# A four-layer graph attention kernel: the adjacency mask turned by DMA, and its value test moved to layer 2

## The chip, the core and the metric

The kernel runs on one core of a Trainium2 chip. The core has a matrix engine (TensorE, PE in the profile), a vector engine (VectorE, DVE), an activation engine (ScalarE, ACT), a general engine (GpSimd, POOL) and a queue engine that only issues transfers (SyncE, SP). Each engine works off its own list of instructions in order, and waits on semaphores where an instruction needs another engine's result. Transfers between the chip's main memory (HBM) and the on-chip memory (SBUF) are done by 16 DMA engines. Matrix products land in a small accumulator memory (PSUM). The metric is the device time of one launch in microseconds (us), the median of several runs.

## What is computed

Sixteen graphs of 1024 nodes with 256 features each pass through four attention layers. All four layers use the same adjacency matrix of its graph. It is symmetric, has ones on its diagonal and is sparse otherwise, with int32 entries of 0 and 1. In a shortened form:

```python
x: (16, 1024, 256) float32;  adj: (16, 1024, 1024) int32
for layer in 0, 1, 2:                       # each with its own W, a
    h = maximum(layernorm(x), 0)
    Wh = h @ W
    e = act(Wh @ a1 [:, :, None] + Wh @ a2 [:, None, :])
    weights = where(adj != 0, exp(+-e), 0); normalised by row
    x = x + post(weights @ Wh)              # post: identity, elu, elu
h = maximum(layernorm(x), 0)                # layer 3: four heads of 64
e_h = leaky_relu(src_h[:, :, None] + dst_h[:, None, :])   # where adj == 1
att = softmax over edges
y = relu(att @ h_h + bias) + h_h; normalised per head, * gamma + beta
x = x + y
```

Layer 3 of the reference has separate vectors for edge types 1 to 5. The fast path of the kernel covers adjacency values of 0 and 1 only. It therefore tests every entry, and a general path, which is compiled into the same program, runs if the test fails.

## The kernel before

**Tiling.** A graph is one batch. Its 1024 nodes are NI = 8 blocks of P = 128 rows; node 128 i + p lies in block i at partition p. The features x_b of a batch stay in SBUF for all four layers.

**The mask.** `load(b)` (L96) prepares a batch. SP loads x_b (L99). For each block i, POOL issues a transfer that loads 128 rows of the adjacency and casts int32 to bf16 on the way (L106). ACT takes (a - 1/2) squared of each entry and sums it by row (L117); a row of only zeros and ones sums to N/4, and a larger sum is found at the end of the kernel (L530 to L532). TensorE then transposes the eight 128x128 squares of the block into a PSUM tile called misc (L122), and ACT copies this to the byte mask (L123). The mask has the sources j at the partitions, in blocks j, and the targets along the row. The matrix is symmetric in this data, but the kernel doesn't use that. The mask is loaded AHEAD = 2 blocks ahead, from a pool of three buffers.

**A layer.** `project` (L233) normalises two node blocks at a time: statistics and subtraction on DVE (L239, L240, L244), the inverse root on POOL (rstd, L227), transposes on TensorE (L252), a copy to SBUF on ACT (hT, L254), then the projection (L259). What comes out is evicted to V by ACT (L320, L322) and DVE (L324), in layer 3 to h3, ex and V3 by ACT and POOL (L340 to L348). `weigh` (L268) makes the attention weights of a layer or head: TensorE spreads one value per node over a row of all partitions (L276), and then one DVE instruction per source block j (L280) compares the row with a value per partition and multiplies by the mask of block j. Exponentials are taken per node and not per edge, so this instruction is all the work there is per edge. `attend` (L352) multiplies weights with V (L367) for each target block i, and its `finish` adds the result to x_b: in layers 1 and 2 by an exponential on ACT (L303), three DVE instructions (L295, L296, L305, L306 in all) and an addition on POOL (L307). Layer 3 multiplies per head in halves of 512 targets (L471), copies the sums (L481), transposes them (L486), and normalises y per head on DVE, ACT and POOL (L431 to L446). The output leaves by SP (L502).

**The order of the work.** Everything is written as Python generators, and each `yield` hands a planned cost back. Two streams exist, one of the even and one of the odd batches. The loop at L520 always continues the stream with the smaller sum; the second begins LAG = 120 units later. So a batch's layers interleave with those of another batch, which is about half a batch away. Inside layer 3 of batch b, `next(coming)` (L482) takes one step of `load(b + 2)` after each half of a head. On top of this written order, the build places instructions on each engine by its own estimate of when they become ready, so that an engine's list can differ from the order of the code. Once built, the lists are fixed.

The few lines that set the loads' place are these:

```python
        for i in range(AHEAD):
            fetch(i)
        yield
        for i in range(NI):
            if i + AHEAD < NI:
                fetch(i + AHEAD)
            adj_i = fetched.pop(i)
            ...
            yield
```

Of the kernel before, what the change touches and what calls it, by code (L numbers as in the profile page):

```python
# [32 lines left out]
F32 = mybir.dt.float32  # L33
BF = mybir.dt.bfloat16
U8 = mybir.dt.uint8
I16 = mybir.dt.int16
I32 = mybir.dt.int32
AF = mybir.ActivationFunctionType
ALU = mybir.AluOpType
AX = mybir.AxisListType  # L40

P = 128
# [17 lines left out]
def short_path(ctx: ExitStack, tc: tile.TileContext, ins: dict, out: bass.AP, bad: bass.AP):  # L60

    nc = tc.nc
    x, adj = ins["x"], ins["adj"]
    B, N, D = x.shape
    H, T, E = ins["L3_a_src"].shape
    NI = N // P
    NK = D // P
    HALF = 512
    NH = N // HALF
    NG = HALF // P  # L70
    EXT = [3, 3, 3, 3 * H]
    AHEAD = 2
    LAG = 120.0

    const = ctx.enter_context(tc.tile_pool(name="const", bufs=1))
    nodes = ctx.enter_context(tc.tile_pool(name="nodes", bufs=3))
    adjs = ctx.enter_context(tc.tile_pool(name="adjs", bufs=3))
    wide = ctx.enter_context(tc.tile_pool(name="wide", bufs=2))
    psum = ctx.enter_context(tc.tile_pool(name="psum", bufs=2, space=bass.MemoryType.PSUM))

    ident = const.tile([P, P], F32, name="ident")
    make_identity(nc, ident)
    ident_b = const.tile([P, P], BF, name="ident_b")
    nc.vector.tensor_copy(ident_b, ident)
    minus_half = const.tile([P, 1], F32, name="minus_half")
    nc.vector.memset(minus_half, -0.5)
    ones = const.tile([P, P], F32, name="ones")
# [2 lines left out]
    squares = const.tile([P, B, NI], F32, name="squares")  # L90
    inverses = const.tile([P, B, NI], F32, name="inverses")


    xs, masks = {}, {}

    def load(b: int):  # L96

        xs[b] = nodes.tile([P, NI, D], F32, name="x_b")
        nc.sync.dma_start(xs[b], x[b].rearrange("(i p) f -> p i f", p=P))  # L99
        mask = masks[b] = nodes.tile([P, NI, N], U8, name="mask")  # L100
        fetched = {}

        def fetch(i: int):

            fetched[i] = adjs.tile([P, N], BF, name="adj_i")
            nc.gpsimd.dma_start(fetched[i], adj[b, ts(i, P), :])  # L106

        for i in range(AHEAD):
            fetch(i)
        yield  # L110
        for i in range(NI):
            if i + AHEAD < NI:
                fetch(i + AHEAD)
            adj_i = fetched.pop(i)

            every = wide.tile([P, N], BF, name="wide")
            nc.scalar.activation(  # L117
                every, adj_i, AF.Square, bias=minus_half, accum_out=squares[:, b, i : i + 1]
            )
            turned = psum.tile([P, NI, P], BF, name="misc")  # L120
            for j in range(NI):
                nc.tensor.transpose(turned[:, j, :], adj_i[:, ts(j, P)], ident_b)  # L122
            nc.scalar.copy(mask[:, :, ts(i, P)], turned)  # L123
            yield

    edges = ctx.enter_context(tc.tile_pool(name="edges", bufs=NI))
# [8 lines left out]
    bias = const.tile([P, D], F32, name="bias")  # L135
# [94 lines left out]
    def accumulator(b: int) -> bass.AP:  # L230
        return psum.tile([P, HALF], F32, name=f"acc{b % 2}")
# [36 lines left out]
    def weigh(b: int, column, c, op, into: list):  # L268


        while row_taken:
            yield 0.25
        row_taken.append(b)
        r = psum.tile([P, N], F32, name="row", bufs=1)
        for i in range(NI):
            nc.tensor.transpose(r[:, ts(i, P)], column(i).to_broadcast([P, P]), ident)  # L276
        yield 0.5
        for j in range(NI):
            w = edges.tile([P, N], F32, name=f"weights{b % 2}")
            nc.vector.scalar_tensor_tensor(w, r, c(j), masks[b][:, j, :], op0=op, op1=ALU.mult)  # L280
            into.append(w)
            if j == NI - 1:
                row_taken.pop()
            yield 0.5

    def start(behind, b: int):

        for t in behind:
            if row_taken == [b]:
                return  # L290
            yield t
# [17 lines left out]
    def batch(b: int):  # L309
        xb = xs.pop(b)  # L310
        if b == 0:
            next(preparing)
        coming = load(b + 2) if b + 2 < B else iter(())

        def begin(l: int):

            V = nodes.tile([P, NI, H, E + 1], F32, name="V", bufs=4).rearrange("p i h e -> p i (h e)")

            def evict(i: int, projected: bass.AP, rstd: bass.AP):
                nc.scalar.activation(V[:, i, D : D + 3], projected[:, D:], AF.Exp, scale=rstd)  # L320
                if l == 2:
                    nc.scalar.mul(V[:, i, :D], projected[:, :D], rstd)  # L322
                else:
                    nc.vector.tensor_scalar(  # L324
                        V[:, i, :D], projected[:, :D], rstd, V[:, i, D : D + 1],
                        op0=ALU.mult, op1=ALU.mult,
                    )

            return V, evict

# [3 lines left out]
        def begin3():  # L334
            h3 = last["h3"] = single.tile([P, NI, D], F32, name="h3")
            V3 = nodes.tile([P, NI, H, E + 1], F32, name="V", bufs=4)
            ex = last["ex"] = small.tile([P, NI, 3 * H], F32, name="ex", bufs=2)
# [14 lines left out]
        def attend(l: int, V: bass.AP, finish, then: int):  # L352

            weights = []
            behind = weigh(
                b, lambda i: V[:, i, D + 2 : D + 3], lambda j: V[:, j, D + 1 : D + 2],
                ALU.min if l == 1 else ALU.max, weights,
            )
            yield from start(behind, b)
            following = begin(then) if then < 3 else begin3()  # L360
            steps = iter(())
            accs = {}

            def product(i: int, j: int):
                if j == 0:
                    accs[i] = accumulator(b)[:, : D + 1]
                nc.tensor.matmul(  # L367
                    accs[i], weights[j][:, ts(i, P)], V[:, j, : D + 1],
                    start=(j == 0), stop=(j == NI - 1),
                )  # L370


            for j in range(NI):
                next(behind)
                product(0, j)
                product(1, j)
                yield 0.9
            for _ in behind:
                pass
            for i in range(NI):  # L380
                if i > 1:
                    for j in range(NI):
                        product(i, j)
                acc = accs.pop(i)
                finish(i, acc)
                if i != 0:
                    yield 3.6
                if i % 2 == 1:

                    yield from steps  # L390
                    steps = project(b, then, xb, i // 2, following[1])
                yield from islice(steps, 1)
            yield 1.0
            yield from steps
            return following[0]
# [8 lines left out]
        def finish(i: int, acc: bass.AP):  # L404
            add_elu(xb[:, i, :], acc)
# [6 lines left out]
        for steps in pairs:  # L412
            yield from steps
        if b == 0:
            for _ in chain(loading, preparing):
                pass
        V = yield from attend(0, V, finish0, 1)
        V = yield from attend(1, V, finish, 2)
        V3 = yield from attend(2, V, finish, 3)


        h3, ex = last["h3"], last["ex"]
        y = single.tile([P, NI, H, E], F32, name="y")
        normed = []
        shape = [P, NI, E]

        def center(h: int):

            yh = y[:, :, h, :]
            head = ts(h, E)  # L430
            nc.gpsimd.tensor_add(yh, yh, bias[:, head].unsqueeze(1).to_broadcast(shape))  # L431
            nc.vector.scalar_tensor_tensor(yh, yh, 0.0, h3[:, :, head], op0=ALU.max, op1=ALU.add)
            mean = small.tile([P, NI], F32, name="mean")
            nc.vector.tensor_reduce(mean, yh, AX.X, ALU.add)
            nc.vector.tensor_scalar_mul(mean, mean, 1.0 / E)
            nc.vector.tensor_sub(yh, yh, mean.unsqueeze(2).to_broadcast(shape))
            square = wide.tile(shape, F32, name="wide")
            nc.scalar.activation(square, yh, AF.Square)
            var = small.tile([P, NI], F32, name="var")
            nc.vector.tensor_reduce(var, square, AX.X, ALU.add)  # L440
            return yh, head, inverse_root(var, NI, L3_EPS, 1.0 / E)
# [18 lines left out]
        for n in range(H * NH):  # L460
            h, g = divmod(n, NH)
# [37 lines left out]
            pass  # L499
        rescale(*normed.pop())  # L500
        for g in range(NH):
            nc.sync.dma_start(  # L502
                out[b, ts(g, HALF), :].rearrange("(i p) f -> p i f", p=P),
                y[:, ts(g, NG)].rearrange("p i h e -> p i (h e)"),
            )
        yield 1.0

# [1 line left out]
    def stream(first: int):  # L509
# [3 lines left out]
        for b in range(first, B, 2):  # L513
            yield from batch(b)

    loading, preparing = load(0), prepare()
    next(loading)
    next(preparing)
    streams = [[0.0, stream(0)], [LAG, stream(1)]]
    while streams:  # L520
        ahead = min(streams, key=lambda s: s[0])
        t = next(ahead[1], None)
# [381 lines left out]
```

## Time and profile before

| what | value |
|---|---|
| median of three runs | 3197.18 us (3196.29 to 3198.49) |
| the profiled execution's own time | 3197.01 us |
| its span, first to last instruction | 3195.3 us |
| mean granted TensorE clock | 0.991 |
| DMA moved | 72.09 MB, mean 23 GB/s |
| HBM read, written | 86.38 MB, 16.78 MB |
| L122 TensorE, mask transposes | 1024 x, 84.2 us busy, 222 ns each |
| L117 ACT, Square of a block | 128 x, 1142 ns and 190 ns for the sum's read-out |
| L123 ACT, mask copies | 128 x, 1011 ns |
| L106 POOL, issue of a load | 128 x, 605 ns; 3.8 us from issue to landing |
| L280 DVE, weights | 896 x, 1275 ns |

How to read it: the page gives the busy time of each engine over the span, and then groups of equal instructions by line with their mean time. A group is followed by the time in which its engine stood idle just before it, and by what ended that idle time. An engine's busy share is an average over stages with different limits. Matmuls are pipelined, so that the durations of single ones overlap.

### The profile page before, as it was taken

The page shows a single profiled execution, that of the slowest core. Times are in us where ns is not written, and L with a number is a line of the kernel's source. Part 1 is how long each engine was busy: PE and PEld are TensorE (multiplying, and loading weights), DVE is VectorE, ACT ScalarE, POOL GpSimd, SP SyncE. Part 2 cuts the span into 40 slices and gives each one's busy share as a digit, 9 for nine tenths or more (in the row PEclk, how much of TensorE's full clock was granted, in tenths as well). Part 3 has the DMA queues.
Part 4 walks back from the last instruction along what each step waited for, and adds up shares of the span by engine and source line. Part 5 has one row for each costly group of instructions (what it writes and reads, how often), then busy time and mean ns, then how long its engine had stood idle before and what let it go on. Part 6 is the DMA issues. An engine that isn't in the chain of part 4 may idle for free.

```text
span 3195.3 us, 37581 instructions
## 1 busy us (share of the span) xinstructions
PE 3058.6 (96%) x13702; PEld 2112.1 (66%) x13702; DVE 2370.9 (74%) x5244; ACT 855.3 (27%) x1857; POOL 1002.4 (31%) x1286
## 2 busy tenths in 40 slices
PE   7899999999999999999999999999999999999987
PEld 5666776667666686666867667676676767766552
DVE  5576778777787767787687876878768787677756
ACT  3322223222232312323123231232313222232120
POOL 1223324232242322423224232342323323233332
PEclk8999999999999999999999999999999999999998
DMA  4101101111010100101001010111101111000000
GB/s 107 24 7 17 34 4 21 34 20 30 7 37 18 28 19 11 44 11 43 1 14 40 14 40 1 17 37 17 37 1 20 34 17 37 4 14 14 1 14 14
DMA packets 55951, 72.09 MB, mean 23 GB/s; under 512 B 5072, under 2 KB 38992, under 8 KB 55760
## 3 DMA queue, kind: packets, MB, share of 16 engines
q0 software_dynamic: 18432, 33.56, 6.9%
q1 hardware_dynamic: 37328, 36.05, 3.5%
q8 instruction: 111, 1.82, 0.2%
q14 instruction: 80, 0.66, 0.1%
HBM read 86.38 MB, written 16.78 MB: 32 GB/s over the span
## 4 chain that ended last, share of the span: by engine, by line
PE 71%; DVE 17%; POOL 6%; ACT 2%; issue 2%; DMA 1%; ACTq 0%; POOLq 0%; SPq 0%; DVEq 0%
PE acc L367 32%; PE acc L471 21%; PE acc L259 12%; DVE weights L280 8%; PE misc L252 2%; PE row L276 2%; POOL rstd L227 2%; POOL y L431 1%; POOL x_b L307 1%; PE misc L122 1%; DVE centered L244 1%; DVE stats L239 1%; DVE above L305 1%; ACT below L303 1%; PE misc L486 1%
## 5 line engine op out<-in xcount | busy, mean ns | idle before, releaser
L367 PE MATMUL acc<-V,weights 128*128 128x257 f32 x6144 | 1449.8, 384 | 41.9 <-DVE weights L280 20.3
L367 PEld LDWEIGHTS acc<-V,weights 128*128 128x128 f32 x6144 | 1143.8, 191 | 352.3 <-DVE weights L280 99.4
L471 PE MATMUL acc<-weights,V 128*65 128x512 f32 x2048 | 960.6, 593 | 1.9 <-DVE weights L280 1.7
L280 DVE SCALAR_TENSOR_TENSOR weights<-row,ex,mask 128x1024 f32<-128x1024 f32 x512 | 626.9, 1275 | 18.7 <-PE row L276 11.3
L259 PE MATMUL acc<-W,hT 128*128 128x259 f32 (+1 forms) x2048 | 521.7, 392 | 38.0 <-ACT hT L254 22.8
L471 PEld LDWEIGHTS acc<-weights,V 128*65 128x65 f32 x2048 | 272.4, 138 | 354.3 <-issue 311.5
L227 POOL TENSOR_TENSOR rstd<-rstd,minus_half 128x2 f32<-128x2 f32 (+1 forms) x320 | 301.0, 943 | 645.6 <-DVE rstd L226 632.0
L280 DVE SCALAR_TENSOR_TENSOR weights<-row,V,mask 128x1024 f32<-128x1024 f32 x384 | 474.5, 1275 | 33.4 <-PE row L276 32.9
L259 PEld LDWEIGHTS acc<-W,hT 128*128 128x128 f32 x2048 | 378.4, 191 | 170.7 <-ACT hT L254 60.0
L307 POOL TENSOR_TENSOR x_b<-x_b,above 128x256 f32<-128x256 f32 x256 | 191.1, 751 | 813.6 <-DVE above L306 731.1
L303 ACT ACTIVATE below<-acc,inv 128x256 f32<-128x256 f32 x256 | 120.3, 474 | 756.3 <-DVE inv L296 553.4
L239 DVE BATCH_NORM_STATS2 stats<-x_b 128x6 f32<-128x256 f32 x512 | 209.3, 416 | 127.6 <-POOL x_b L307 119.5
L254 ACT COPY hT<-misc 128x512 f32<-128x512 f32 x256 | 147.4, 587 | 372.9 <-PE misc L252 372.8
L244 DVE TENSOR_SCALAR centered<-x_b,mv 128x256 f32<-128x256 f32 x512 | 208.6, 411 | 5.2
L324 DVE TENSOR_SCALAR V<-acc,rstd,V 128x256 f32<-128x256 f32 x256 | 135.2, 537 | 74.6 <-ACT V L320 73.6
L106 POOL DMA_DIRECT2D adj_i<-in_adj_dram x128 | 77.4, 605 | 356.9 <-PE misc L122 115.3
L320 ACT ACTIVATE V<-acc,rstd 128x3 f32<-128x3 f32 x384 | 98.9, 262 | 333.8 <-PE acc L259 333.2
L305 DVE TENSOR_SCALAR above<-acc,inv 128x256 f32<-128x256 f32 x256 | 122.0, 482 | 80.5 <-ACT below L303 77.5
L252 PEld LDWEIGHTS misc<-ident,centered 128*128 128x128 f32 x1024 | 124.1, 141 | 77.5 <-issue 41.1
L252 PE MATMUL misc<-ident,centered 128*128 128x128 f32 x1024 | 158.7, 276 | 15.6 <-DVE rstd L226 8.3
L481 ACT COPY sums<-acc 65x512 f32<-65x512 f32 x128 | 74.3, 581 | 346.4 <-PE acc L471 346.1
L123 ACT CAST mask<-misc 128x1024 uint8<-128x1024 bf16 x128 | 129.1, 1011 | 96.4 <-PE misc L122 96.4
(69 smaller groups left out, 2104.9 us busy)
## 6 DMA issues: line engine op xcount, KB each, us to landing
adj_i<-in_adj_dram POOLq DMA_DIRECT2D x128, 256.0 KB, 3.8
x_b<-in_x_dram SPq DMA_DIRECT2D x16, 1024.0 KB, 7.6
out_dram<-y SPq DMA_DIRECT2D x32, 512.0 KB, 3.9
W<-in_L_gnn_W_dram SPq DMA_DIRECT2D x3, 256.0 KB, 8.9
weights<-in_L_gnn_a_dram SPq DMA_DIRECT2D x3, 256.0 KB, 9.0
W<-in_L_gnn_W_dram SPq DMA_DIRECT2D x2, 128.0 KB, 9.3
weights<-in_L_gnn_a_src_dram SPq DMA_DIRECT2D x1, 128.0 KB, 9.2
weights<-in_L_gnn_a_dst_dram SPq DMA_DIRECT2D x1, 128.0 KB, 7.2
```

The source lines that it names most:

```text
L227: nc.gpsimd.tensor_tensor(r, r, minus_half.to_broadcast([P, n]), op=ALU.pow)
L239: nc.vector.bn_stats(stats, xb[:, 2 * pair + n, :])
L244: nc.vector.tensor_scalar(centered[:, n, :], xb[:, 2 * pair + n, :], mv[:, n, 0:1], 0.0, op0=ALU.subtract, op1=ALU.max,)
L252: nc.tensor.transpose(turned[:, k, ts(n, P)], centered[:, n, ts(k, P)], ident)
L254: nc.scalar.copy(hT, turned)
L259: nc.tensor.matmul(projected, hT[:, k, ts(n, P)], W[l][:, k, :], start=(k == 0), stop=(k == NK - 1),)
L280: nc.vector.scalar_tensor_tensor(w, r, c(j), masks[b][:, j, :], op0=op, op1=ALU.mult)
L303: nc.scalar.activation(below, acc[:, :D], AF.Exp, scale=inv)
L305: nc.vector.tensor_scalar(above, acc[:, :D], inv, 0.0, op0=ALU.mult, op1=ALU.max)
L307: nc.gpsimd.tensor_add(xi, xi, above)
L367: nc.tensor.matmul(accs[i], weights[j][:, ts(i, P)], V[:, j, : D + 1], start=(j == 0), stop=(j == NI - 1),)
L471: nc.tensor.matmul(accT, V3[:, j, h, :], weights[h * NI + j][:, ts(g, HALF)], start=(j == 0), stop=(j == NI - 1),)
```

## The change

- **Cast.** `load(b)` no longer brings the adjacency to SBUF. POOL issues four transfers from HBM to HBM that cast 256 rows each from int32 to bytes, into one of two scratch matrices (`narrows`), by the batch's parity. Within 256 rows, the even nodes go to the first 128 rows of the scratch and the odd ones to the next 128.
- **Turn.** SP issues four transposing transfers (`dma_start_transpose`), which move 128 columns of two bytes each of the 1024 scratch rows to a mask tile of 128 partitions. A pair of bytes, an even and an odd node, moves as one element. So partition p of part c holds nodes 256 c + 2 p and the one after it, side by side, and the mask of a source block is read with a step of two bytes (L280's last operand).
- **Blocks.** Node blocks follow this order throughout: x_b and the output are moved by `in_blocks`, in runs of two rows.
- **Test.** The test for 0 and 1 gets a generator of its own, `test(b)`. It loads the bf16 rows once more and squares them in place on ACT. It no longer belongs to layer 3 of batch b - 2: its first step, which issues loads 0 and 1, comes after layer 0 of batch b, and one further step follows each `finish` of layer 2.
- **Places of the steps.** The casts for b + 2 are issued after layer 0 of batch b, right ahead of the test's first step. The turns and the x_b load take the steps in layer 3 that the loads had.
- **Queues.** The x_b loads of batches 2 and later and all output transfers go from SP's queue to POOL's. Casts, test loads and the later turns keep their written order.
- **Buffers.** Rows for the test have four buffers instead of three, and `square` in layer 3 (L437) has one instead of two. The transposes (L122), the mask copies (L123) and the bf16 identity (L83, L84) are gone.

```diff
-    adjs = ctx.enter_context(tc.tile_pool(name="adjs", bufs=3))
+    adjs = ctx.enter_context(tc.tile_pool(name="adjs", bufs=4))
...
+    dram = ctx.enter_context(tc.tile_pool(name="dram", bufs=1, space=bass.MemoryType.DRAM))
...
+    def in_blocks(a: bass.AP) -> bass.AP:
+        return a.rearrange("(c p t) f -> p c t f", p=P, t=2)
...
+    narrows = [dram.tile([N, N // 2], BF, name=f"narrow{n}") for n in range(2)]
 
     def load(b: int):
+        narrow = narrows[b % 2]
+        rows = narrow.bitcast(U8).rearrange("(c t q) j -> c q t j", t=2, q=P)
+        for c in range(NI // 2):
+            cast = nc.gpsimd.dma_start(
+                rows[c], adj[b, ts(c, 2 * P), :].rearrange("(q t) j -> q t j", t=2)
+            )
+            tc.keep_in_program_order(cast)
+        yield
+
+        mask = masks[b] = nodes.tile([P, NI // 2, N, 2], U8, name="mask")
+        for c in range(NI // 2):
+            turn = nc.sync.dma_start_transpose(
+                mask[:, c].rearrange("p n t -> p (n t)").bitcast(BF), narrow[:, ts(c, P)]
+            )
+            if b > 1:
+                tc.keep_in_program_order(turn)
+            yield
         xs[b] = nodes.tile([P, NI, D], F32, name="x_b")
-        nc.sync.dma_start(xs[b], x[b].rearrange("(i p) f -> p i f", p=P))
...
+        queue = nc.gpsimd if b > 1 else nc.sync
+        queue.dma_start(xs[b].rearrange("p (c t) f -> p c t f", t=2), in_blocks(x[b]))
+        yield
+
+    def test(b: int):
+
         fetched = {}
...
+        for i in range(-AHEAD, NI):
             if i + AHEAD < NI:
-                fetch(i + AHEAD)
+                adj_i = fetched[i + AHEAD] = adjs.tile([P, N], BF, name="adj_i")
+                tc.keep_in_program_order(nc.gpsimd.dma_start(adj_i, adj[b, ts(i + AHEAD, P), :]))
+            if i < 0:
+                if i == -1:
+                    yield
+                continue
+
             adj_i = fetched.pop(i)
-            every = wide.tile([P, N], BF, name="wide")
             nc.scalar.activation(
-                every, adj_i, AF.Square, bias=minus_half, accum_out=squares[:, b, i : i + 1]
-            )
-            turned = psum.tile([P, NI, P], BF, name="misc")
-            for j in range(NI):
-                nc.tensor.transpose(turned[:, j, :], adj_i[:, ts(j, P)], ident_b)
-            nc.scalar.copy(mask[:, :, ts(i, P)], turned)
+                adj_i, adj_i, AF.Square, bias=minus_half, accum_out=squares[:, b, i : i + 1]
+            )
             yield
...
-            nc.vector.scalar_tensor_tensor(w, r, c(j), masks[b][:, j, :], op0=op, op1=ALU.mult)
+            nc.vector.scalar_tensor_tensor(w, r, c(j), masks[b][:, j // 2, :, j % 2], op0=op, op1=ALU.mult)
...
+        testing = test(b)
...
                 finish(i, acc)
+                if l == 2:
+                    next(testing)
...
         if b == 0:
-            for _ in chain(loading, preparing):
+            for _ in chain(preparing, loading):
                 pass
         V = yield from attend(0, V, finish0, 1)
+        next(coming, None)
+        next(testing)
         V = yield from attend(1, V, finish, 2)
...
-            nc.sync.dma_start(
-                out[b, ts(g, HALF), :].rearrange("(i p) f -> p i f", p=P),
-                y[:, ts(g, NG)].rearrange("p i h e -> p i (h e)"),
+            nc.gpsimd.dma_start(
+                in_blocks(out[b, ts(g, HALF), :]),
+                y[:, ts(g, NG)].rearrange("p (c t) h e -> p c t (h e)", t=2),
             )
...
     loading, preparing = load(0), prepare()
-    next(loading)
+
+    for _ in islice(loading, 2 + NI // 2):
+        pass
     next(preparing)
```

## The prediction

> **What bounds the kernel now.** I read the page first: engines, slices, chain.
>
> ```profile
> PE 3058.6 (96%) x13702; PEld 2112.1 (66%) x13702; DVE 2370.9 (74%) x5244; ACT 855.3 (27%) x1857; POOL 1002.4 (31%) x1286
> ...
> PE 71%; DVE 17%; POOL 6%; ACT 2%; issue 2%; DMA 1%; ACTq 0%; POOLq 0%; SPq 0%; DVEq 0%
> ```
>
> TensorE is busy for 96% of the span and holds 71% of the chain. Its queue is in order: whatever is late for its next instruction costs the whole kernel, since both streams share that queue. In windows of 160 us its idle time is 32 us in the first, 36 in the last 155, and 70 in the 2880 us between: about 5 us a batch. So time is won by taking work from TensorE and lost by making it wait for ACT, DVE or POOL.
>
> ```profile
> 1014.57 0.61 PE L122 MATMUL misc<-ident_b,adj_i 128*128 128x128 bf16 x8
> 1015.02 0.66 PE L259 MATMUL acc<-W,hT 128*128 128x259 f32 x2
> ```
>
> From the timeline of TensorE: eight mask transposes (L122) hold up the next matmul by 0.45 us, not by 8 x 0.22, because they are pipelined.
>
> ```profile
> q0 software_dynamic: 18432, 33.56, 6.9%
> ...
> adj_i<-in_adj_dram POOLq DMA_DIRECT2D x128, 256.0 KB, 3.8
> ```
>
> All loads that POOL issues are in one queue, q0. Its packets took 6.9% of 3195.3 us = 220 us for 128 loads: 1.72 us of all 16 DMA engines each, of the 3.8 us from issue to landing.
>
> ```profile
> core 0: us, PE busy (x) PEld busy (x) DVE busy (x) ACT busy (x) POOL busy (x), PEclk, DMA share, GB/s
> 157.00:158.00 1.00, 1.00 (x7) 0.76 (x8) 0.19 (x1) 1.00 (x3) 0.72 (x1) 1.00 1.10 199
> ```
>
> The window table shows two such loads back to back at their densest: 199 GB/s written, 1.32 us for 256 KB. So a load costs 1.32 to 1.72 us when others queue ahead of it.
>
> ```profile
> PE acc L259 <- ACT hT L254: 22.8, 28, 1.8
> ...
> PE acc L367 <- ACT h L341: 8.5, 8, 3.0
> ...
> ACT L117 <- DMA adj_i<-in_adj_dram: 9.2, 1, 9.2
> ...
> ACT wide L117 <- DMA adj_i<-in_adj_dram: 8.4, 7, 3.2
> ```
>
> From the waits: TensorE does stand still for copies that ACT makes, and ACT hardly ever waits for adjacency data (17.6 us in all, all in the first two batches). The change touches just this.
>
> **What the skill says.** DMA: Bandwidth & Descriptors, "SWDGE vs HWDGE vs iDMA": casting DMAs are issued by GpSimd alone, transposing ones by SP or ACT alone; so casts and test loads must share q0. The trace agrees as far as it goes (the casting loads are all on q0). The same page, "Queues, rings and completion order": on each DMA engine descriptors of one ring are consumed in order. No wait of before tests this; I rest on it. TensorE: Matmul & The Clock Gate, "Architectural detail": ACT's queue is strictly first in, first out. Nothing in the trace contradicts that. SBUF — State Buffer, "Door 1": a stride is free within a 16-byte line, up to 16 one-byte elements. No read of before is strided so.
>
> **The change, part by part.** The sum is made against the profiled execution's own 3197.0 us (span 3195.3 and 1.7 around it); the median of the runs is 3197.18, so nothing need be shifted.
>
> 1. *Transposes off TensorE.* 128 blocks of eight x 0.445 us = 57 us. The group's busy time, 84.2, is the ceiling; the chain's 1.2% for L122, 38 us, the floor. I take -57.
>
> 2. *Mask copies off ACT* (128 x 1.01 us, L123) and the shared PSUM buffer freed. ACT is at 27%, so this is worth what it takes from TensorE's waits for hT (22.8 us): 0 to -23, taken as -8. ident_b's copy, 0.2 us, is nothing.
>
> 3. *Start.* Now batch 0's eight loads trickle in one by one, the last at 36.7 us in the chain, and the first weights start at 39.16. After, four casts are issued at once. They read 4 MB, which is eight loads' worth: 10.5 to 13.8 us. SP's 3.4 MB beside them takes some 9 us at the 369 GB/s that the window 4 to 6 us shows. So casts end near 25. The turns follow on SP. No turn is in the trace; by the skill's 261 GB/s (DMA page, "Latency and other measured facts") a turn of 256 KB is estimated at 1 us and the 2.1 us of latency that a load shows. First weights near 32, but x and W0 come some 2 us later too. If a turn takes 10 us, the fourth pair of weights is 17 us later than now. -9 to +17, taken as -6. In the later batches turns have over 100 us to spare, since next(coming) issues casts a whole stage ahead; that cover gone, each late turn would stall TensorE by its own length.
>
> 4. *Strided mask reads* (L280, 896 x 1.275 us). Stride 2 lies within the skill's 16[...]. 0; upper end in the rivals.
>
> 5. *Tests behind casts.* This is the new wait. In batch(b) four casts for b+2 are issued, and right after them the test loads 0 and 1 of b, in one ring. A cast reads as much as two loads, so the first test load lands 3.8 + (10.5 to 13.8) = 14.3 to 17.6 us after the first cast's issue (call this c). In the built order of ACT, the two Squares of these loads (1.14 + 0.19 us each) stand far earlier than layer 2: in even batches right behind the hT copy of the last layer-1 pair, before two V evictions; in odd ones behind the first two exponentials of layer 1, before a sums copy; in batch 1 ahead of an hT copy; in batch 0 ahead of those exponentials. What is queued behind on ACT waits until both Squares are done and itself runs: c + 17.3 to 21. Against that, when TensorE needs it, counted from its built order with the intervals of the trace (0.86 us a 65x512 product, 0.43 a 128x257, 0.48 a 128x259) and DVE's 1.275 per weights:
>  - even, b = 2 to 12 (six): row transposes of layer 1, eight weights and four V rows later, c + 12. Late by 5 to 9, 7 x 6 = 42.
>  - odd, b = 3 to 13 (six): transposes of the sums, c + 12. Late by 5.5 to 9, 7.3 x 6 = 44.
>  - b = 1: projection from hT, c + 9: 10. b = 0: c is 80.75 (rstd at 80.04 + 0.7), the exponential is wanted at 95.13, and is free at 98 to 101: 4.5.
>  Sum 100, ends 74 and 126. TensorE idles 5 us a batch anyway, and some of that falls into these waits: I take +90.
>
> 6. *Later tests.* Load i+2 is issued on POOL behind step i's x_b addition, and its Square stands one or two places later on ACT. Exp to landing is 0.47 + 0.92 + 0.75 + 0.57 + 3.8 = 6.5 us (L303, L305 with L306, L307, issue, landing) while the next exponential is wanted 4 to 8 us on. Output and x loads, moved to the same ring, are 1 MB a batch each (2.7 us each at 380 GB/s) ahead of some. 0 to 7 us a batch over 16, so 0 to 112; I take 3 x 15 = +45.
>
> 7. *POOL's issues.* 64 casts, 32 outputs and 14 x loads at 0.6 us (L106's 128 rows) to 1.2 (256 rows) = 66 to 105 us more on an engine at 31%; rstd (L227) queued behind four casts comes up to 5 us late. In return bufs=4 takes away POOL's waits for freed buffers (L106: 357 us idle). SP's queue, now of turns, holds nothing else in the steady state, so a turn's wait for its mask buffer hurts nobody. The output's end is issued from POOL instead of SP, 0.3 us later (two issues at 0.6 against 0.46). 0 to +15, taken as +4.
>
> Sum: -57 - 8 - 6 + 0 + 90 + 45 + 4 = +68, so 3197.0 + 68 = **3265 us**; own range 3210 to 3320.
>
> **Rivals.**
> A, *the tests don't stall TensorE* (0.25; the other side). Place: the two Squares behind the casts. If a cast takes under about 2 us, the first load lands by c + 11 to 12 and the waits shrink into idle time that is there anyway. Then -57 - 8 - 6 + 4 + some 20 = 3150. For it: ACT's own waits for data are 17.6 us now. Against: those loads have nothing ahead of them.
> B, *slow turns* (0.10). A turn of 20 us makes the first masks 40 us late, batch 1's 20, and fills all 16 DMA engines for 80 us of each batch's 200, which doubles the test loads' latency there: 3265 + 60 + some 20 = 3345. Nothing of before shows a turn, so this can't be excluded.
> C, *strided reads cost* (0.05). At half speed 896 x 1.07 us more make DVE 3330 us busy: it becomes the bound, at about 3500. Against: part 4.
> That the change leaves the transposes or tests in place is excluded: the built order holds no transpose of adj_i, 128 Squares as before, 64 casts and 64 turns.
>
> **How the numbers follow.** The main case has 0.60 and gives the forecast. Changes below about 0.2% (6 us) can't be told from none here. Faster: nearly all of A, 0.25. Within 0.2%: A and the main case where they meet, 0.05. Slower: 0.70. The range that should hold 8 in 10 goes from 3145 (half of A left out, 0.12) to 3340 (most of B and C left out, 0.08).
>
> **What would show it.** Parts 1 and 2: no L122, PE busy near 2975 us, ACT's copies gone. Part 5: in the waits of ACT, Squares waiting for adj_i, some 5 to 14 us at a time once a batch, and TensorE idle on hT, V or sums by 5 to 10 us at about 14 places. Part 6: shorter such waits, up to 4 us. Part 3: first weights between 30 and 37 us. Part 4: L280 at 1.275 us. I am wrong if ACT waits less than 100 us in all for adjacency (then A), or if weights wait for turns (then B).

## The result and the profile after

| | before | after |
|---|---|---|
| median | 3197.84 us (3196.29 to 3199.09) | 3331.75 us (3329.3 to 3334.43) |
| ratio, 95% interval | | 1.0419 (1.0401 to 1.0437) |
| profiled span | 3195.3 us | 3328.1 us |
| mean granted TensorE clock | 0.991 | 0.967 |
| TensorE busy, and idle (span less busy) | 3058.6, 136.7 us | 3057.1, 271.0 us |

The change is slower by 134 us; the forecast was 68. Lines of the kernel after are 18 to 23 higher than before for the code named here: L298 is the former L280, L277 was L259, L386 was L367, L494 was L471, L272 was L254, L339 was L320. L106 is the cast, L132 the test load, L139 the Square.

First the page: engines, chain, queue q0 and the issues of loads (count, size, median us to landing).

```profile
PE 3057.1 (92%) x12678; PEld 2091.6 (63%) x12678; DVE 2386.2 (72%) x5243; ACT 737.2 (22%) x1729; POOL 1079.7 (32%) x1396
...
q0 software_dynamic: 44256, 81.80, 14.7%
...
PE 53%; DVE 18%; POOL 10%; DMA 9%; issue 6%; ACT 4%; ACTq 0%; POOLq 0%; SPq 0%; DVEq 0%
...
adj_i<-in_adj_dram POOLq DMA_DIRECT2D x128, 256.0 KB, 3.9
narrow<-in_adj_dram POOLq DMA_DIRECT2D x64, 256.0 KB, 8.7
...
mask<-narrow SPq DMA_TRANSPOSE x64, 3.8
```

1024 TensorE instructions are gone, and yet TensorE is busy as long as before. Its share of the chain falls from 71% to 53%, and DMA, which had 1%, has 9%: TensorE now often waits, and transfers end the wait.

Next the waits of TensorE, and of ACT (total us, times, longest us), with the wait of before that corresponds to the first line.

```profile
PE acc L494 <- DVE weights L298: 48.7, 9, 8.2
PE acc L277 <- ACT hT L272: 48.2, 38, 8.9
PE acc L277 <- DVE above L323: 43.5, 15, 3.4
PE misc L270 <- DVE centered L262: 30.1, 22, 2.9
PE misc L509 <- ACT sums L504: 21.0, 14, 2.8
```

```profile
PE acc L471 <- DVE weights L280: 1.7, 2, 1.5
```

```profile
ACT adj_i L139 <- DMA adj_i<-in_adj_dram: 417.6, 106, 11.7
```

ACT waited 17.6 us in all for adjacency before, and now 417.6 us in 106 waits. How that reaches TensorE is seen in the timeline after layer 0 of batch 2 (start, duration, engine and line, operation; in brackets the idle time ahead and what ended it).

```profile
420.27 1.47 POOL L106 DMA_DIRECT2D narrow<-in_adj_dram  x2
...
424.62 1.10 POOL L132 DMA_DIRECT2D adj_i<-in_adj_dram  x2
...
428.29 3.59 PE L494 MATMUL acc<-weights,V 128*65 128x512 f32 x8
...
434.92 1.15 ACT L139 ACTIVATE adj_i<-adj_i,minus_half 128x1024 bf16<-128x1024 bf16 x1 [11.12 <-DMA adj_i<-in_adj_dram]
...
437.35 0.24 ACT L339 ACTIVATE V<-acc,rstd 128x3 f32<-128x3 f32 x1
437.63 0.55 DVE L343 TENSOR_SCALAR V<-acc,rstd,V 128x256 f32<-128x256 f32 x1 [0.73 <-ACT V L339]
438.08 3.66 DVE L298 SCALAR_TENSOR_TENSOR weights<-row,ex,mask 128x1024 f32<-128x1024 f32 x3
...
439.51 6.63 PE L494 MATMUL acc<-weights,V 128*65 128x512 f32 x8 [7.63 <-DVE weights L298]
```

The first cast is issued at 420.27, the first test load has landed at 434.92, 14.65 us later (forecast: 14.3 to 17.6). ACT's list holds that Square ahead of a V eviction. DVE waits for this eviction with its own V row, and three weights of the other stream stand behind that row. So TensorE, which has nothing of its own to wait for, is idle for 7.63 us. The eight matmuls behind the stall then take 6.63 us, where the eight of the same shape ahead of it took 3.59. The window table shows why (PEclk is the last but two of the columns).

```profile
core 0: us, PE busy (x) PEld busy (x) DVE busy (x) ACT busy (x) POOL busy (x), PEclk, DMA share, GB/s
...
430.00:435.00 5.00, 1.88 (x5) 0.41 (x3) 0.00 (x0) 0.08 (x1) 0.00 (x0) 1.00 1.09 153
435.00:440.00 5.00, 0.49 (x1) 0.30 (x2) 2.92 (x4) 2.59 (x6) 0.00 (x0) 0.53 0.02 3
440.00:445.00 5.00, 5.00 (x7) 1.39 (x6) 1.75 (x2) 0.00 (x0) 0.00 (x0) 0.50 0.00 0
```

From the middle of the stall on, TensorE is granted half clock; the clock records show it from 435.33 to 445.57 us. The Trainium skill says so (TensorE: Matmul & The Clock Gate, "Part 1: The HAM clock gate"): a window of about 3.4 us without activity throttles TensorE to half its rate, until a busy window has passed. The trace agrees for this stall, with clocks of 0.53 and 0.50. Over the whole span the records lose 108 us of full clock, 76 of them while TensorE is busy, against 30 and 16 before. That is where the busy time went that the missing transposes had won.

### The profile page after: what moved, and what is told of

Its sections match the earlier page's. It is cut to its first block, busy times and chain, and to the rows that moved or that the text cites. A ratio compares the mean times of both kernels' runs of the same rounds, so it can differ in the third digit from the quotient of the medians.

```text
span 3328.1 us, 35492 instructions
## 1 busy us (share of the span) xinstructions
PE 3057.1 (92%) x12678; PEld 2091.6 (63%) x12678; DVE 2386.2 (72%) x5243; ACT 737.2 (22%) x1729; POOL 1079.7 (32%) x1396
## 4 chain that ended last, share of the span: by engine, by line
PE 53%; DVE 18%; POOL 10%; DMA 9%; issue 6%; ACT 4%; ACTq 0%; POOLq 0%; SPq 0%; DVEq 0%
PE acc L386 26%; PE acc L494 15%; DMA adj_i<-in_adj_dram 9%; PE acc L277 9%; DVE weights L298 7%; POOL rstd L245 2%; POOL x_b L325 2%; PE misc L270 2%; DVE above L323 2%; POOL y L454 1%; ACT below L321 1%; DVE stats L257 1%; POOL narrow L106 1%; PE row L294 1%; ACT adj_i L139 1%
## 5 line engine op out<-in xcount | busy, mean ns | idle before, releaser
L386 PE MATMUL acc<-V,weights 128*128 128x257 f32 x6144 | 1452.0, 386 | 27.1 <-DVE above L323 11.5
L386 PEld LDWEIGHTS acc<-V,weights 128*128 128x128 f32 x6144 | 1159.8, 192 | 341.8 <-issue 81.4
L494 PE MATMUL acc<-weights,V 128*65 128x512 f32 x2048 | 979.7, 602 | 49.1 <-DVE weights L298 48.7
L298 DVE SCALAR_TENSOR_TENSOR weights<-row,ex,mask 128x1024 f32<-128x1024 f32 x512 | 627.2, 1275 | 15.9 <-PE row L294 11.6
L277 PE MATMUL acc<-W,hT 128*128 128x259 f32 (+1 forms) x2048 | 547.0, 408 | 96.5 <-ACT hT L272 48.2
L277 PEld LDWEIGHTS acc<-W,hT 128*128 128x128 f32 x2048 | 397.3, 200 | 238.9 <-ACT hT L272 81.5
L494 PEld LDWEIGHTS acc<-weights,V 128*65 128x65 f32 x2048 | 276.3, 140 | 412.5 <-issue 368.5
L298 DVE SCALAR_TENSOR_TENSOR weights<-row,V,mask 128x1024 f32<-128x1024 f32 x384 | 475.2, 1275 | 57.7 <-PE row L294 57.7
L139 ACT ACTIVATE adj_i<-adj_i,minus_half 128x1024 bf16<-128x1024 bf16 x128 | 146.9, 1147 | 429.4 <-DMA adj_i<-in_adj_dram 417.6
L272 ACT COPY hT<-misc 128x512 f32<-128x512 f32 x256 | 148.3, 584 | 389.0 <-PE misc L270 389.0
L262 DVE TENSOR_SCALAR centered<-x_b,mv 128x256 f32<-128x256 f32 x512 | 217.7, 428 | 4.8
L454 POOL TENSOR_TENSOR y<-y,bias 128x512 f32<-128x512 f32 x64 | 81.9, 1279 | 401.7 <-DVE y L512 358.0
L339 ACT ACTIVATE V<-acc,rstd 128x3 f32<-128x3 f32 x384 | 97.9, 261 | 385.5 <-PE acc L277 384.3
```

The lines of the kernel that those rows point to most:

```text
L139: nc.scalar.activation(adj_i, adj_i, AF.Square, bias=minus_half, accum_out=squares[:, b, i : i + 1])
L262: nc.vector.tensor_scalar(centered[:, n, :], xb[:, 2 * pair + n, :], mv[:, n, 0:1], 0.0, op0=ALU.subtract, op1=ALU.max,)
L277: nc.tensor.matmul(projected, hT[:, k, ts(n, P)], W[l][:, k, :], start=(k == 0), stop=(k == NK - 1),)
L298: nc.vector.scalar_tensor_tensor(w, r, c(j), masks[b][:, j // 2, :, j % 2], op0=op, op1=ALU.mult)
L386: nc.tensor.matmul(accs[i], weights[j][:, ts(i, P)], V[:, j, : D + 1], start=(j == 0), stop=(j == NI - 1),)
L494: nc.tensor.matmul(accT, V3[:, j, h, :], weights[h * NI + j][:, ts(g, HALF)], start=(j == 0), stop=(j == NI - 1),)
```

## The experiments

Differences are to the median of the kernel before, measured beside each run (3197.3 to 3198.5 us). Unless said otherwise, each run is the change with the edit shown; `...` marks lines left out.

**Tests ahead of the casts.**

```diff
-        next(coming, None)
         next(testing)
+        next(coming, None)
```

> The changed kernel with one swap: after layer 0 the test's loads 0 and 1 are issued ahead of the four casts and not behind them. Theory 1 (the two Squares stand still behind the casts in one ring, ACT's queue stands behind them, and TensorE then also loses clock): the windows of 30 us around these places in the changed kernel hold 92 us of TensorE idle and 28 us of lost clock, some 10 of it usual, so 110 less: 3215 to 3250, with no wait of a first Square above 4 us. Rival 2 (the later tests in layer 2 cost nearly all): 3310 to 3330, since these keep their waits. Rival 3 (the traffic of casts and turns itself, or POOL's longer list, is what costs): within 10 of 3332, wherever the loads stand.

Measured: 3256.24 us, ratio 1.018 (1.0163 to 1.0197), +58; 76 of the 134 us are gone. That is 6 us less than theory 1 had at its range's end. ACT still waits 335.6 us for adjacency:

```profile
ACT adj_i L139 <- DMA adj_i<-in_adj_dram: 335.6, 108, 7.0
```

The first Square of a batch now waits about 2 us in even batches, but about 6 in most odd ones, where theory 1 allowed 4. So the casts in the ring cost much, but four fifths of what ACT waits have another cause. Rival 3 falls: the traffic is the same.

**Without the test; with resident Squares; before without transposes.** Three bounds. In the first the test loads and Squares are deleted:

```diff
-                adj_i = fetched[i + AHEAD] = adjs.tile([P, N], BF, name="adj_i")
-                tc.keep_in_program_order(nc.gpsimd.dma_start(adj_i, adj[b, ts(i + AHEAD, P), :]))
...
-            nc.scalar.activation(
-                adj_i, adj_i, AF.Square, bias=minus_half, accum_out=squares[:, b, i : i + 1]
-            )
```

> The changed kernel without the test: no test loads and no Squares, and the sums that the Squares would give are filled with 0 once. This leaves the test for 0 and 1 out. Theory 1 and rival 2 together (all of the loss is ACT waiting for the test's data): 3331.8 - 110 (first tests) - 90 (later tests: 97 us of idle in the windows of layer 2, 19 of it usual, and 13 of lost clock) = 3130, 3095 to 3140 with the lost clock elsewhere; below the kernel before. Rival 3 (casts, turns, strided masks): it stays above 3250.

In the second the Square reads and writes tiles of its own, and nothing reads the loaded rows, whose pool has two buffers instead of four:

```diff
-                adj_i, adj_i, AF.Square, bias=minus_half, accum_out=squares[:, b, i : i + 1]
+                every, resident, AF.Square, bias=minus_half, accum_out=squares[:, b, i : i + 1]
```

> The changed kernel with all its test loads, but the Squares read a tile that is resident, so ACT does the work of the test and waits for no data; the test is left out in effect. Theory 1 with rival 2: as without the test, plus at most what 128 loads' issue on POOL and 170 us of ACT's work cost: 3100 to 3160. Rival 3 (traffic on the ring): above 3250, as the traffic is that of the changed kernel.

In the third, the kernel before loses L120 to L123, and all batches read one mask of ones:

```diff
-            turned = psum.tile([P, NI, P], BF, name="misc")
-            for j in range(NI):
-                nc.tensor.transpose(turned[:, j, :], adj_i[:, ts(j, P)], ident_b)
-            nc.scalar.copy(mask[:, :, ts(i, P)], turned)
```

> The kernel before without the mask transposes and mask copies: its loads and Squares stay, and all batches read one mask tile filled with ones. This leaves out the use of the adjacency. It measures steps 1 and 2 of the forecast by themselves: -57 and -8, so 3132; floor -38 (3159), ceiling -84 and -23 (3090). If the transposes were hidden by TensorE's usual idle time, 3180 or more.

Measured: without the test 3159.57 (ratio 0.9881, 0.9864 to 0.9897), -39; resident 3180.6 (0.9948, 0.9931 to 0.9964), -18; before without transposes 3149.04 (0.9849, 0.9833 to 0.9865), -49. With all loads, but nobody waiting for them, the change is faster than before; so it is waiting for data that makes it slower, not the traffic. But each of the three won less than I expected. The first two lie 20 us beyond their ranges' ends: something outside the test costs too. And the resident run differs by more than the wait, as one line of its source view shows (count, shortest, median and longest duration in ns, first and last start in us):

```profile
L142 ACT ACTIVATE every<-resident,minus_half x128: 1136/1148/1197, 2.2 to 201.1; 128x1024 bf16<-128x1024 bf16 x128
```

All 128 Squares, of 16 batches, ran in the first 201 us. So the build moved them as far forward as their data allowed, wherever they are written; I saw what that means only later.

**Other places and more lead for the test.** Three versions, meant to let the loads land in time: the test's steps in the batch's own layer 3; AHEAD = 3 with the tests first; and the test in layer 3 once more, with AHEAD = 3, spread casts and SP's queue for output and x_b (the last diff below).

```diff
-                if l == 2:
-                    next(testing)
...
-        next(testing)
...
         behind = weigh3(0)
+        next(testing)
...
+            next(testing)
             next(coming, None)
```

> The changed kernel with the test's steps back at the half-head steps of layer 3 (of the batch's own layer 3), and no test step after layer 0 or in layer 2. The output is complete. Theory 1 (what costs is ACT waiting for data that were asked for too late): most waits go, and the time falls from 3332 towards the 3180.6 of the run whose Squares wait for no data; but the third load of a batch is issued behind the other stream's four casts, so that one Square a batch may still wait some 10 us: 3180 to 3250. Rival (any place of the test costs, since ACT's 1.3 us per Square is what delays TensorE): no better than the 3256 of the run with the tests first.

```diff
-    AHEAD = 2
+    AHEAD = 3
```

> Tests ahead of the casts as in the first run, and each later test load one finish earlier (AHEAD 3 with the same four buffers). The output is complete. Step 6 of the forecast (a load is landed 6.5 us after the exponential, and the next is wanted 4 to 8 us on): one finish is about 4 us of TensorE, so nearly all later waits (2.9 us in the mean, 7 at most) go: 3256 falls by some 60 of the 75.6 that lie between it and the run with resident Squares, to 3185 to 3210. Rival (POOL's issue, not the lead, delays the chain from the exponential to the next projection): 3245 to 3260.

```diff
+                if l == 1 and i % 2 == 1:
+                    next(coming, None)
...
-        queue = nc.gpsimd if b > 1 else nc.sync
+        queue = nc.sync
...
-            nc.gpsimd.dma_start(
+            nc.sync.dma_start(
```

> A version meant to keep what the change gains: test steps in the batch's own layer 3 with loads three blocks ahead, one cast after every second finish of layer 1 and not four at once, and output and x_b loads on SP's queue again. The output is complete. If the terms add up: 3149 (the run without transposes) to 3165, faster than the kernel before by 1 to 1.5%. If casts in the ring still hold up a test load, or SP's turns hold up the output: 3180 or more.

Measured: 3302.94 (1.0329, 1.0312 to 1.0346), 3259.22 (1.0187, 1.017 to 1.0204) and 3259.0 (1.0191, 1.0174 to 1.0208). All three missed what they were meant to reach, and each lies where its rival put it; but ACT still waits 445, 292 and 351 us for adjacency, and the runs with a pin below, which keep ACT's Squares, POOL's issues, the casts and SP's turns, leave none of these rivals as the main cause. Step 6 of the forecast, too short a lead, falls with this: a load that is issued one finish earlier wins nothing. The timeline of the run with AHEAD = 3 shows why.

```profile
1206.85 1.15 POOL L132 DMA_DIRECT2D adj_i<-in_adj_dram  x2
...
1210.90 1.15 ACT L139 ACTIVATE adj_i<-adj_i,minus_half 128x1024 bf16<-128x1024 bf16 x1 [2.20 <-DMA adj_i<-in_adj_dram]
...
1213.82 0.56 ACT L272 COPY hT<-misc 128x512 f32<-128x512 f32 x1
...
1214.44 0.70 PE L277 MATMUL acc<-W,hT 128*128 128x259 f32 x2 [2.65 <-ACT hT L272]
```

The first Square is written behind the first finish of layer 2, a whole layer after its load. In ACT's built list it stands ahead of the next hT copy. It waits there for the landing and runs 4 us after its load's issue; TensorE then waits for hT. Here the Square has moved forward with its load, so the longer lead did not help it.

**The Square pinned.** One call added to the change keeps the build from moving the Square ahead of the ACT instruction that is written before it.

```diff
-            nc.scalar.activation(
+            square = nc.scalar.activation(
                 adj_i, adj_i, AF.Square, bias=minus_half, accum_out=squares[:, b, i : i + 1]
             )
+            tc.keep_in_program_order(square)
```

> The changed kernel with one edit: each Square is pinned on ACT behind the ACT instruction that is written ahead of it (an exponential of layer 2). The loads stay where they are, 0 and 1 behind the four casts. The output is complete. New theory (the build's estimate has a load landed sooner than the chip does, so it puts the Square into ACT's list right behind the load's issue, wherever the step is written; then it doesn't matter how far ahead loads are issued, as the runs with loads three ahead and with the test in layer 3 showed): the first two Squares now stand some 60 us behind their loads and wait for nothing, casts ahead or not; later ones stand one or two finishes behind theirs. The time falls towards the 3180.6 of the run with resident Squares: 3180 to 3215, where loads 2 and 3 may still be late. First theory as I stated it (the place of the test loads behind the casts in the ring is what costs): 75 us of loss stay, so 3250 or more.

Measured: 3165.08 us, ratio 0.9898 (0.9882 to 0.9915): 167 us faster than the change, 33 faster than before, and below the range that I had set, which the resident run had given. Part of that difference is the crowd of Squares at the resident run's start: its TensorE is busy for 164.8 of the first 200 us, here for 170.7. The rest wasn't traced. The run without any test is only 5.5 us faster, and the two intervals overlap. The casts stand ahead of the test loads as in the change. My first theory, that this place in the ring is what costs, falls in that form. ACT's waits for adjacency are down to one:

```profile
ACT adj_i L139 <- DMA adj_i<-in_adj_dram: 0.4, 1, 0.4
```

The same place of batch 2 in its timeline (lines are one higher than after from L139 on):

```profile
403.61 1.47 POOL L106 DMA_DIRECT2D narrow<-in_adj_dram  x2
...
407.96 1.10 POOL L132 DMA_DIRECT2D adj_i<-in_adj_dram  x2
...
409.29 0.26 ACT L340 ACTIVATE V<-acc,rstd 128x3 f32<-128x3 f32 x1 [2.15 <-PE acc L278]
...
411.62 7.03 PE L495 MATMUL acc<-weights,V 128*65 128x512 f32 x16
```

The V eviction runs as soon as its product is done, and TensorE's 16 matmuls are without a gap, at 0.44 us each. The two Squares run at 511.17 and 512.66, a hundred us after their loads.

```profile
PE 3003.5 (95%) x12678; PEld 2067.3 (65%) x12678; DVE 2378.7 (75%) x5243; ACT 728.6 (23%) x1729; POOL 1078.2 (34%) x1396
...
PE 68%; DVE 20%; POOL 7%; ACT 2%; issue 2%; SPq 1%; DMA 0%; ACTq 0%; POOLq 0%; DVEq 0%
```

The page shows the price of the stalls in both its parts. Against the change, TensorE's busy time is 53.6 us less with the same instructions, and its idle time 156.9 instead of 271.0. The clock records account for nearly all of the first part: the clock lost while TensorE is busy falls from 76 to 26 us.

**POOL's issues.** What is left of the missing gain? In the run with resident Squares, POOL's timeline shows the two output issues right ahead of the x_b addition from which TensorE's next projection follows (lines are three higher than after):

```profile
933.27 1.32 POOL L472 TENSOR_TENSOR y<-y,x_b 128x512 f32<-128x512 f32 x1
...
934.89 1.54 POOL L528 DMA_DIRECT2D out_dram<-y  x2 [0.30 <-POOL y L472]
...
936.45 0.73 POOL L328 TENSOR_TENSOR x_b<-x_b,above 128x256 f32<-128x256 f32 x1
...
939.63 2.96 PE L280 MATMUL acc<-W,hT 128*128 128x259 f32 x6 [4.42 <-DVE above L326]
```

In the run of before without transposes, whose SP issues the output, the wait at this place is shorter by 1.64 us (lines are two lower than before):

```profile
936.22 4.15 PE L257 MATMUL acc<-W,hT 128*128 128x259 f32 x10 [2.78 <-DVE above L303]
```

The edit that puts output and x_b loads back on SP's queue (the last two pieces of the last diff but one) was tried with resident Squares, and with pinned ones with AHEAD = 2 and 3.

> The run with resident Squares (which leaves the test out in effect), but output and x_b loads are issued by SP again and not by POOL. In the trace of that run the two output issues (1.54 us together) stand on POOL between the last product with x_b and the x_b addition that TensorE's next projection waits for (4.42 us of idle there, against 2.78 in the run without transposes). Theory (step 7 was priced too low because these issues stand on the path): 16 x 1.54 and 14 x up to 0.79, so 20 to 35 less: 3145 to 3161. Rival (the issues are hidden, as step 7 said): 3172 to 3182.

> The changed kernel with the Squares pinned (3165.1) and output and x_b loads on SP's queue, loads two blocks ahead as in the change. The output is complete. It tells apart what made the run with both further edits 27 us faster (3138.2). If it was POOL's issues on the path to the next projection: 3132 to 3145, since ACT waits for adjacency for 0.4 us in all when the Squares are pinned, so that a third load ahead has nothing left to win. If the loads ahead had a part: 3148 to 3158, with the 14 us that the same edit was worth with resident Squares.

> The changed kernel with the Squares pinned in written order, loads three blocks ahead, and output and x_b loads on SP's queue. The output is complete. New theory: the 3166.4 of the run with resident Squares and SP's queue, as no Square waits any more: 3155 to 3175, faster than the kernel before by about 1%. If Squares or loads behind an exponential still hold up the chain to the next projection: 3185 to 3215.

Measured: 3166.4 with resident Squares (0.9899, 0.9882 to 0.9915), 14 less than without the edit and less than I expected; 3146.32 with pinned ones (0.9844, 0.9826 to 0.9861), 19 less; 3138.24 with AHEAD = 3 besides (0.9814, 0.9798 to 0.9831). The second lies just outside the lower of its two expectations: the issues have most of the 27 us. TensorE's waits for `above` ahead of a projection and for the centred rows, both behind POOL's x_b additions, are 13.3 us shorter with the edit (58.2 and 44.9 in the two pinned runs). That these transfers leave the ring of the casts is hardly the cause, since ACT waits 0.4 us for adjacency and DVE 0.4 for a mask without the edit; the shares of output and x_b loads are not told apart. The remaining 8 (the two intervals just touch) go with AHEAD = 3, though Squares wait for 0.4 us in all in the one run and not at all in the other. The one wait of TensorE that differs much is that for the centred rows, 21.7 us with AHEAD = 2 and 9.9 with AHEAD = 3:

```profile
PE misc L271 <- DVE centered L263: 21.7, 19, 3.1
```

```profile
PE misc L271 <- DVE centered L263: 9.9, 13, 3.1
```

Those rows depend on POOL's x_b additions, so that the place of the load issues among these is a likely cause. It wasn't tested apart.

**The version in layer 3, pinned.** Its one edit against the run of 3259.0 us is the pin.

> The earlier version with the test in layer 3, casts spread over layer 1 and SP's queue (3259.0), with the Squares pinned in written order as the only further edit. The output is complete. New theory: the Square now stands behind the copy of the sums of its own step, three steps of some 8 us behind its load, so the 351 us of ACT's waits for adjacency shrink to below 40: 3150 to 3180. If it was the casts between the test loads in the ring that held up the Squares: above 3220.

Measured: 3138.41 us (0.981, 0.9793 to 0.9826), 121 less by the pin alone, with no wait of ACT for adjacency. Both places of the test are equally good once the Square stays there (3138.24 and 3138.41). Either version is 1.9% faster than the kernel before.

## Why the prediction held in sign, and was 66 us short

The measured 3331.75 lies above the 3320 to which the main case went, and inside the wider range to 3340. The sum can be rebuilt from pairs of runs:

| step | forecast | measured | between |
|---|---|---|---|
| 1 and 2, transposes and copies | -65 | -49 | before and before without transposes |
| 7, POOL's issues | +4 | +18 to +19 | pinned, with SP's queue and without |
| 3, 4 and the rest | -6 | -2 | what remains to the pinned run's -33 |
| 5, tests behind casts | +90 | +76 | the change and tests first |
| 6, later tests (and what the first still wait) | +45 | +91 | tests first and pinned |
| sum | +68 | +134 | |

1. *Transposes.* TensorE's busy time is 54.7 us less without them (3058.6 to 3003.9), close to the 57. What the sum lacked is idle time: it grows from 136.7 to 142.7 us, as what DVE owes is late next. The wait for `above` ahead of a projection is 8.3 us before and 25.1 in the run without transposes.
2. *Mask copies.* Nothing: TensorE's wait for hT is 22.8 us before, 32.2 in that run, 22.9 with pinned Squares. The -8 failed.
3. *Start.* The first weights start at 30.3 us instead of 39.1 (forecast: near 32), the first product with them at 31.64 instead of 40.41. Turns take 3.8 us to landing, so rival B falls. What the start is worth is not separated. Part of it is in the first row, since without transposes the first weights already start at 35.0; against that run, the pinned kernel is 3.8 us ahead where layer 3 of batch 0 begins (195.1 and 198.9 us).
4. *Strided reads.* 1275 ns as before: exactly 0, rival C falls.
5. *Tests behind casts.* Landing and place were right: windows of 30 us around the 14 places hold 92 us of idle and 31 of clock lost while TensorE is busy, and the swap returns 76, of which 53 are idle time. That the size came near +90 is in part luck. In the six odd batches from 3 on, TensorE waits 4.2 to 4.6 us at this place, where I had 7.3, and lost clock made up for it. The victim was not always the one that I named; in even batches it was DVE's weights for the other stream (7.4 to 8.2 us each).
6. *Later tests.* This step failed in mechanism, and its +45 is half of what was measured, within its own 0 to 112. It took the wait for a short lead between exponential and landing. The runs with AHEAD = 3 and in layer 3 refute that: the Square is put so soon behind its load in ACT's list that it waits, whatever the lead. Its waits on ACT go to 6.8 us, where I had 4. The same holds for step 5, which took the built place of the Squares as given and blamed what stood ahead of their loads. With the Squares pinned the waits of both steps are gone (0.4 us).
7. *POOL's issues.* Priced at +4 as hidden behind an engine at 31%. They are not hidden: the output's two issues, 1.54 us, stand at the one place of the batch where POOL is on the path.

The sum had no term for the clock, and this is its largest gap. Steps 5 and 6 together had TensorE stand idle for 135 us. The pin takes 114 us of its idle time away, so the waits were not sized too small; it also takes 53.6 us of busy time, for which the sum had nothing. For the same reason TensorE's busy time is 3057.1 us and not near the 2975 that was named as a sign. For the stall shown, the price is its 7.63 us and 3.0 more, half of the 6.1 us that TensorE then works at half clock. So the waits were 21 us shorter than forecast; against this stand the 53.6 us, the 16 that steps 1 and 2 gave less, and the 14 that step 7 cost more.

Shown are the early place and the effect of the pin. That the build takes a load to be landed sooner than the chip lands it is argued from these; its own numbers were not looked at.

## What to carry to other kernels

An instruction that waits for a transfer blocks its whole engine at the place where the *built* list has it, which may be far from where it is written. If lead time doesn't cure such a wait, pin the consumer, before moving the loads. And where an engine feeds TensorE's next stage, price a DMA issue by who stands behind it, not by the engine's busy share.

## What was not expected of the hardware

- One stall of 7.63 us costs 3.0 us more in the products behind it (6.63 against 3.59 us for eight matmuls). Shorter idle stretches bring half clock too: TensorE waits 1.78 us until 694.23 and 2.78 until 698.21, and the clock records of the kernel after show half clock for 3.41 us from 698.15 on. A whole window of 3.4 us without activity, as the page on the clock gate has it, was not needed here.
- A cast of 256 rows from HBM to HBM takes 8.7 us to land (5.8 to 18.0), four at a time in one queue. The test load behind four casts landed 10.3 us after its own issue (14.65 after the first cast's); the median of all test loads is 3.9.
- A transposing transfer of 256 KB lands 3.8 us after its issue, and the byte mask read with a step of two costs DVE nothing.
